# A Perceiver block on one core: first residual's norm folded into centered weights, table roots in the last batch, and side steps in another order

## The chip, the core and the metric

The kernel runs on one core of a Trainium2 chip. The metric is the device time of one execution in microseconds (us). The engines are named as in the profile: PE multiplies matrices (PEld loads its weights, beside it), DVE is the vector engine, ACT the scalar engine with its function tables, POOL and SP issue little work here beside DMAs. All data are 32-bit floats.

## The reference, cut to what matters

There are four batches of 256 tokens with 256 channels, and a context of 4096 tokens with 192 channels for each batch.

```
x = x + xattn(layernorm(x), ctx)    # 16 heads of 16, 256 queries against 4096 keys
x = x + attn(layernorm(x))          # 16 heads, q and k normed per head, causal softmax, 256 x 256
x = x + ffn(layernorm(x))

attn(h): k, q, v = h @ Wk.T, h @ Wq.T, h @ Wv.T, cut into heads
         q, k = headnorm(q)*g + b, headnorm(k)*g + b   # (t - mean) * rsqrt(var + 1e-5) over a head's 16
         softmax(q k^T / 16, causal) @ v @ Wo.T + bo
ffn(h):  logits = (gelu([h, slot_mean] @ w1 + b1) @ w2 + b2) / (|tau| + 0.1)
         alpha = softmax over the best 8 of 64 slots, 0 elsewhere
         si = (alpha^T h) / (sum of alpha + 1e-8)        # 64 slots x 256
         S = GRU(si, slots)                              # gates r, z, n
         y = S + softmax(q k^T / 8) v                    # attention of the 64 slots, one head
         (alpha @ (norm(y) @ wvp)) @ wo + bo
layernorm(x): (x - mean) / sqrt(var + 1e-5) over 256 channels
```

## The kernel before

`fast_` keeps a hand-written order for PE, DVE and ACT; each engine runs its instructions as written and stalls where an operand is late. The eight PSUM banks are four pairs (`two`), and each slot takes them in rotation as `w, x_, y, z`.

The loop runs over `b` from 0 to 4. For b = 0 to 3 it walks the context of batch b in slots `p`, each of which handles two blocks of 128 keys: `cross_block` multiplies keys with queries (L181) into the four pairs and takes the exponentials on ACT (L1666 and L1668), and one step later `cross_weigh` multiplies them with the values (L195) and DVE adds the result to `sums` (L1680). While batch b is in cross attention, all that follows cross attention for batch b-1 runs as side work: the dictionary `plan[b, p, i]` puts a function into slot p at one of five places, and `take(i, ...)` calls it with PSUM banks. Functions that `yield` go on at the next `later()`. Slot 6 of each batch from 1 on is the self attention (`SELF_AT`): two `self_block` calls and no cross attention. Slots 4 to 14 of b = 0 hold the weights' preparation (`set_plain` and so on). Even slots prepare the next keys, odd ones the next values.

At b = 4 there is no cross attention left. The side work of batch 3 runs alone, step after step, and the last steps of batch 2 (`slot_mix`, `slot_values`, `give`) stand among it. So that PE is not idle there, `fill` issues multiplications of zeros (L1052) whose number is set in `WAITS`: for each slot, us ahead of `take(1)` and us at the slot's end, at 0.43 us each.

Steps that the change touches:

- `cross_out` adds the first residual; its continuation is `norm` (statistics L958 and L959, then `rsqrt`, then the application L965). `rsqrt` is a bit trick (L943) and three Newton rounds of three instructions (L947 to L949), all on DVE. `x1_turned` transposes the normed x1 on PE (L980) and copies it on DVE (L986); `qk` multiplies it with the weights (L992), copies it and squares it on ACT, sums the squares on DVE (L1291), takes the roots and scales the heads (L1300). `qk_turned` transposes (L1318) and applies gain and offset on DVE (L1327, L1338). `self_values` copies its product on DVE (L166).
- `self_block` takes exponentials (L1703) and multiplies each tile's diagonal with the causal mask on DVE (L1705), right behind them.
- `normed_x` of the next batch stands at slot 5, `queries` at slot 14, with both halves in one bank.
- `routing` finds the best eight on DVE (L1393, L1394) and takes exponentials (L1399); `gates` are the GRU's products (L992) and elementwise work; `slot_qkv`, `slot_scores`, `at_turned` stand at slots 14, 15, 16; `slot_mix` (L1515, L1523, L1525), `slot_values` (product L992, then L1545) and `give` (L1551, L1559, output DMA L1560) at slots 5, 6 and 9 of the batch after, and behind the loop for batch 3.

Of the kernel before, what the change touches and what calls it, by code (L numbers as in the profile page):

```python
# [20 lines left out]
P = 128  # L21
# [11 lines left out]
CLAMP = 10000.0  # L33
MASKED = -1e30
# [11 lines left out]
    1: (0.4, 4.3),  # L46
    2: (0.4, 0.0),
    3: (0.0, 5.2),
    6: (0.0, 0.43),
    7: (0.0, 0.86),  # L50
    8: (0.4, 2.6),
    9: (0.0, 0.43),
    10: (0.0, 0.43),
    11: (0.0, 2.6),
    12: (0.0, 0.43),
    13: (0.0, 1.7),
    15: (0.0, 0.86),
}

# [853 lines left out]
def fast_(es, tc, nc, a, out, k, const, x0):  # L913
# [23 lines left out]
    def rsqrt(v):  # L937

        p, n = v.shape
        y = small.tile([P, n], F32, name="rs_y", tag=f"rs_y{n}")[0:p]  # L940
        t = small.tile([P, n], F32, name="rs_t", tag=f"rs_t{n}")[0:p]
        nc.vector.tensor_scalar(v, v, EPS, None, ALU.add)
        nc.vector.tensor_scalar(  # L943
            y.bitcast(I32), v.bitcast(I32), -0.5, 1597463007.0, ALU.mult, ALU.add
        )
        for _ in range(3):
            nc.vector.scalar_tensor_tensor(t, y, -0.5, y, ALU.mult, ALU.mult)  # L947
            nc.vector.tensor_tensor(t, t, v, ALU.mult)
            nc.vector.scalar_tensor_tensor(y, t, 1.5, y, ALU.add, ALU.mult)  # L949
        return y  # L950

    def norm(src):
# [7 lines left out]
        nc.vector.tensor_copy(var, mv[:, :, 1])  # L960
        rs = rsqrt(var)
# [54 lines left out]
    def queries(s, bank):  # L1016


        for c in range(2):
            product(  # L1020
                bank[:, c * NQ : (c + 1) * NQ],
                lambda m: k.wq[:, m, c * P : (c + 1) * P],
                lambda m: s.xnT[:, m, :],
            )
        qh = qp.tile([P, 2, 2, NQ], F32, name="qh", tag="qh")
        for c in range(2):
            q = bank[:, c * NQ : (c + 1) * NQ]
            nc.vector.tensor_scalar(
                qh[:, c, 0, :], q, k.bq[:, c : c + 1], pscale[:, 0:1], ALU.add, ALU.mult
            )  # L1030
            nc.scalar.activation(
                qh[:, c, 1, :], q, AF.Identity, bias=bqodd[:, c : c + 1], scale=pscale[:, 1:2]
            )
        s.qh = qh.rearrange("p c e q -> p c (e q)")
# [3 lines left out]
    for b, s in enumerate(batches):  # L1038
        s.b = b
# [78 lines left out]
    def set_plain(bank):  # L1118
# [13 lines left out]
        for v in vself:  # L1132
            ones_beside(nc, v)

# [93 lines left out]
    def set_centered(bank):  # L1228

        nc.vector.memset(sumto, 1.0 / C)  # L1230
# [27 lines left out]
    def cross_out(s, bank):  # L1258
# [9 lines left out]
        apply = norm(x1)  # L1268
        yield
        yield  # L1270
        s.x1n = halves(temp())
        apply(s.x1n)
        nc.gpsimd.tensor_tensor(x1, x1, abo.unsqueeze(1).to_broadcast([P, QT, C]), ALU.add)

    def x1_turned(s, bank):
        s.x1nT = turned(bank, s.x1n)
        s.qk = [temp() for _ in range(QT)]
        s.var = small.tile([P, QT * 2 * H], F32, name="var", tag="var")

    def qk(s, t, bank):  # L1280
        product(
            bank,
            lambda c: s.x1nT[:, c, t * P : (t + 1) * P],
            lambda c: wqkv[:, c, 0 : 2 * C],
        )
        nc.scalar.copy(s.qk[t], bank)
        sq = temp()
        nc.scalar.activation(sq, bank, AF.Square)
        yield
        var = s.var[:, t * 2 * H : (t + 1) * 2 * H]  # L1290
        nc.vector.tensor_reduce(var, sq.rearrange("p (h d) -> p h d", d=D), AX.X, ALU.add)  # L1291
        if t == 1:
            nc.vector.tensor_scalar(s.var, s.var, 1.0 / D, None, ALU.mult)
            rs = rsqrt(s.var)
            yield
            yield
            for u in range(QT):
                f = s.qk[u].rearrange("p (h d) -> p h d", d=D)
                r = rs[:, u * 2 * H : (u + 1) * 2 * H]
                nc.vector.tensor_tensor(  # L1300
                    f, f, r.unsqueeze(2).to_broadcast([P, 2 * H, D]), ALU.mult
                )

    def self_values(s, bank):
        for t in range(QT):
            product(
                bank[:, t * C : (t + 1) * C],
                lambda c: s.x1nT[:, c, t * P : (t + 1) * P],
# [3 lines left out]
        spread_values(nc.vector.tensor_copy, s.vself, halves(bank))  # L1312

    def qk_turned(s, i, bank):

        for c in range(2):
            for t in range(QT):
                nc.tensor.transpose(  # L1318
                    bank[:, (2 * c + t) * P : (2 * c + t + 1) * P],
                    s.qk[t][:, i * C + c * P : i * C + (c + 1) * P],  # L1320
# [3 lines left out]
        if i == 0:  # L1324
            q = held.tile([P, 2, 2, NQ], F32, name="sq", tag="sq", bufs=1)
            for e in range(2):
                nc.vector.tensor_scalar(  # L1327
                    q[:, :, e, :],
                    src,
                    gb[:, e : e + 1],  # L1330
                    gb[:, 2 + e : 3 + e],
                    ALU.mult,
                    ALU.add,
                )
            s.sq = q
        else:
            s.sk = held.tile([P, 2, NQ], F32, name="sk", tag="sk", bufs=1)
            nc.vector.tensor_scalar(s.sk, src, gb[:, 4:5], gb[:, 5:6], ALU.mult, ALU.add)  # L1338
# [6 lines left out]
    def self_out(s, bank):  # L1345
# [9 lines left out]
        apply = norm(s.x2)  # L1355
# [14 lines left out]
    def routing(s, bank):  # L1370

        for t in range(QT):
# [7 lines left out]
        lg, rest, best = (  # L1380
            small.tile([P, QT, n], F32, name=name, tag=name)
            for name, n in (("lg", SLOTS), ("rest", SLOTS), ("best", 8))
# [9 lines left out]
        for t in range(QT):  # L1392
            nc.vector.max(best[:, t, :], lg[:, t, :])  # L1393
            nc.vector.match_replace(rest[:, t, :], best[:, t, :], lg[:, t, :], -3.0e38)  # L1394
        nc.vector.tensor_scalar(top, best[:, :, 0], -1.0, None, ALU.mult)
        yield
        for t in range(QT):
            for x, acc in ((lg, None), (rest, None), (best, asum[:, t : t + 1])):
                nc.scalar.activation(  # L1399
                    x[:, t, :], x[:, t, :], AF.Exp, bias=top[:, t : t + 1], accum_out=acc  # L1400
# [3 lines left out]
        nc.vector.tensor_tensor(lg, lg, rest, ALU.subtract)  # L1404
# [38 lines left out]
    def gates(s, bank, other):  # L1443

        for i, to in ((0, bank), (2, other), (1, other)):
            for m in range(2):
                product(
# [426 lines left out]
```

## Time and profile before

| | |
|---|---|
| three timed runs | 903.44, 904.85, 906.26 us, median 904.85 |
| the profiled execution's own time | 904.43 us |
| its span, first to last instruction | 902.6 us |
| PE busy | 866.2 us, 96% of the span |
| ACT busy | 592.1 us, 66% |
| DVE busy | 328.8 us, 36% |
| last product with values of batch 3 ends | about 819 us |
| last result written by DVE | 895.95 us |

Busy time of PE counts the multiplications of zeros too. The stretch up to about 820 us is the four batches' cross attention with side work; the stretch from there to the end is batch 3's side work alone. An instruction of the small kind (a column or two of 128 rows) takes 0.15 to 0.18 us on DVE, and the next begins about 0.2 us after it.

### The profile page before, as it was taken

The page shows a single profiled execution, that of the slowest core. Times are in us where ns is not written, and L with a number is a line of the kernel's source. Part 1 is how long each engine was busy: PE and PEld are TensorE (multiplying, and loading weights), DVE is VectorE, ACT ScalarE, POOL GpSimd, SP SyncE. Part 2 cuts the span into 40 slices and gives each one's busy share as a digit, 9 for nine tenths or more (in the row PEclk, how much of TensorE's full clock was granted, in tenths as well). Part 3 has the DMA queues.
Part 4 walks back from the last instruction along what each step waited for, and adds up shares of the span by engine and source line. Part 5 has one row for each costly group of instructions (what it writes and reads, how often), then busy time and mean ns, then how long its engine had stood idle before and what let it go on. Part 6 is the DMA issues. An engine that isn't in the chain of part 4 may idle for free.

```text
span 902.6 us, 18933 instructions
## 1 busy us (share of the span) xinstructions
PE 866.2 (96%) x8143; PEld 467.1 (52%) x8143; DVE 328.8 (36%) x872; ACT 592.1 (66%) x838; POOL 18.0 (2%) x21
## 2 busy tenths in 40 slices
PE   8999999999999999999998999999999999998884
PEld 5444545545454555545444545545545545545663
DVE  3134222223346423223346423222445333224753
ACT  3777766766776787676774778767776678662310
POOL 1000000000000100000000000000000000000000
PEclk9999999999999999999999999999999999999997
DMA  7502110000000000000000000000000000000000
GB/s 194 122 25 60 36 48 25 25 20 6 24 24 25 25 25 24 25 25 21 5 25 24 25 29 10 23 25 25 24 25 25 10 27 25 1 1 1 1 12 17
DMA packets 21757, 25.71 MB, mean 28 GB/s; under 512 B 6496, under 2 KB 13216, under 8 KB 21664
## 3 DMA queue, kind: packets, MB, share of 16 engines
q1 hardware_dynamic: 20992, 23.88, 9.3%
q8 instruction: 66, 1.08, 0.5%
q10 hardware_dynamic: 576, 0.52, 0.2%
q14 instruction: 27, 0.22, 0.1%
q0 software_dynamic: 96, 0.01, 0.0%
HBM read 23.35 MB, written 1.05 MB: 27 GB/s over the span
## 4 chain that ended last, share of the span: by engine, by line
PE 89%; DVE 6%; ACT 3%; issue 1%; ACTq 0%; DVEq 0%
PE banks L181 28%; PE banks L195 25%; PE banks L992 8%; PE banks L96 6%; PE banks L123 6%; PE banks L136 4%; PE banks L102 4%; ACT prob L1668 2%; PE banks L980 1%; PE banks L1052 1%; PE banks L1722 1%; PE banks L1693 1%; PE banks L210 1%; DVE prob L1705 1%; PE banks L1415 1%
## 5 line engine op out<-in xcount | busy, mean ns | idle before, releaser
L1668 ACT ACTIVATE prob<-banks 128x1024 f32<-128x1024 f32 x384 | 366.6, 1043 | 0.0
L181 PE MATMUL banks<-qh,kt 32*128 32x512 f32 x2048 | 271.0, 623 | 3.3 <-ACT prob L1668 1.8
L195 PE MATMUL banks<-prob,v 128*32 128x256 f32 x4096 | 234.3, 381 | 2.8 <-ACT prob L1668 1.9
L1666 ACT ACTIVATE prob<-banks 128x512 f32<-128x512 f32 x256 | 139.0, 595 | 134.4 <-PE banks L181 134.4
L195 PEld LDWEIGHTS banks<-prob,v 128*32 128x32 f32 x4096 | 126.5, 110 | 126.8 <-ACT prob L1666 46.0
L181 PEld LDWEIGHTS banks<-qh,kt 32*128 32x128 f32 x2048 | 105.8, 184 | 122.8 <-issue 72.5
L1680 DVE TENSOR_TENSOR sums<-banks,sums 128x512 f32<-128x512 f32 x120 | 82.6, 690 | 200.9 <-PE banks L195 180.0
L123 PE MATMUL banks<-wv,ctx 128*128 128x256 f32 x256 | 62.3, 386 | 0.2
L96 PE MATMUL banks<-ctx,wk 128*128 128x512 f32 x128 | 61.4, 602 | 0.0
L123 PEld LDWEIGHTS banks<-wv,ctx 128*128 128x128 f32 x256 | 46.1, 190 | 13.1 <-ACT prob L1666 4.4
L166 DVE COPY v<-banks 128x512 f32<-128x512 f32 x35 | 23.9, 690 | 77.4 <-PE banks L136 77.4
L110 DVE TENSOR_SCALAR kt<-banks,bk 128x512 f32<-128x512 f32 x32 | 24.0, 750 | 53.3 <-PE banks L102 53.3
L111 ACT ACTIVATE kt<-banks,bk 128x512 f32<-128x512 f32 x32 | 22.0, 687 | 31.1 <-PE banks L102 30.9
L1703 ACT ACTIVATE prob<-banks 128x512 f32<-128x512 f32 (+1 forms) x40 | 24.1, 691 | 21.0 <-PE banks L1693 21.0
L166 ACT COPY v<-banks 128x512 f32<-128x512 f32 x29 | 17.0, 586 | 31.7 <-PE banks L136 31.1
L1052 PE MATMUL banks<-idle 128*128 128x256 f32 x134 | 34.8, 406 | 2.2 <-DVE idle L1047 1.5
L136 PE MATMUL banks<-wv,ctx 64*128 64x256 f32 x256 | 36.3, 402 | 0.0
L102 PE MATMUL banks<-ctx,wk 64*128 64x512 f32 x128 | 36.1, 641 | 0.0
L96 PEld LDWEIGHTS banks<-ctx,wk 128*128 128x128 f32 x128 | 21.3, 190 | 18.5 <-ACT prob L1668 10.6
L1052 PEld LDWEIGHTS banks<-idle 128*128 128x128 f32 x134 | 26.3, 205 | 7.0 <-DVE idle L1047 1.5
L136 PEld LDWEIGHTS banks<-wv,ctx 64*128 64x128 f32 x256 | 22.0, 186 | 11.3 <-issue 9.9
L986 DVE COPY tmp<-banks 128x512 f32<-128x512 f32 x21 | 14.5, 691 | 31.2 <-PE banks L980 30.0
(213 smaller groups left out, 555.0 us busy)
## 6 DMA issues: line engine op xcount, KB each, us to landing
ctx<-in_ctxT SPq DMA_DIRECT2D x32, 256.0 KB, 3.1
ctx<-in_ctxT SPq DMA_DIRECT2D x64, 128.0 KB, 3.3
x<-in_x SPq DMA_DIRECT2D x4, 256.0 KB, 4.1
out<-tmp SPq DMA_DIRECT2D x4, 256.0 KB, 2.5
wih<-in_ffn_WihT SPq DMA_DIRECT2D x1, 768.0 KB, 6.6
tmp<-in_ffn_WhhT SPq DMA_DIRECT2D x3, 256.0 KB, 4.7
wq<-in_L_xattn_Wq ACTq DMA_DIRECT2D x1, 256.0 KB, 4.0
wo<-in_L_xattn_Wo SPq DMA_DIRECT2D x1, 256.0 KB, 4.9
```

Source lines behind the costliest of these rows:

```text
L96: nc.tensor.matmul(pk[c], k.wk[:, 0, c * P : (c + 1) * P], cx[:, 0, :], start=True, stop=False)
L102: nc.tensor.matmul(pk[c], k.wk[left(c), 1, c * P : (c + 1) * P], cx[left(c), 1, :], start=False, stop=True,)
L123: nc.tensor.matmul(pv[n // 2][:, n % 2, :], cx[:, 0, n * P : (n + 1) * P], k.wv[:, 0, :], start=(n % 2 == 0), stop=False, skip_group_check ...
L136: nc.tensor.matmul(pv[u][:, i, :], cx[left(u), 1, n * P : (n + 1) * P], k.wv[left(u), 1, :], start=False, stop=True, skip_group_check=True,)
L166: copy(v[:, :, 0 : H * VW].rearrange("p i (h w) -> p i h w", w=VW)[:, :, :, 0:D], src.rearrange("p i (h d) -> p i h d", d=D),)
L181: nc.tensor.matmul(sc[:, m, :], kt[r, c, i * P : (i + 1) * P], qh[r, c, :], start=True, stop=True)
L195: nc.tensor.matmul(po[q * 32 : (q + 1) * 32, s * NQ : (s + 1) * NQ], v[:, i, w0 : w0 + 32], pr[s][:, m, e * NQ : (e + 1) * NQ], start=(fir ...
L992: nc.tensor.matmul(dst, lhs(c), rhs(c), start=(c == 0), stop=(c == 1))
L1052: nc.tensor.matmul(bank[:, 0:NQ], idle[:, 0:P], idle[:, 0:NQ], start=True, stop=True)
L1666: nc.scalar.activation(pt[:, m, :], sc[:, m, :], AF.Exp)
L1668: nc.scalar.activation(pt, sc, AF.Exp)
L1680: nc.vector.tensor_tensor(s.sums[c], po[:, c, :], s.sums[c], ALU.add)
```

## The change

The first residual is no longer normed ahead of its products. `set_inputs`, new in slot 5 of b = 0, takes each column's mean off the query, key and value weights, so that a row's mean drops out of the products. What is left of the norm is one factor per row: in q and k it cancels against the heads' norm if that norm's epsilon is scaled by the row's variance (`epsx`), and in v it is applied where the values are copied (`rs1`). `x1_turned` therefore transposes x1 itself. The statistics and the Newton rounds are still taken, in `cross_out`.

In the last batch the roots of the heads' norm, the norm of x2 and the slots' norm come from ACT's table (`AF.Sqrt`, then a reciprocal on DVE).

The squares are taken before the copy; the second half of q's gain, k's gain and the values' copy go to ACT. The masks move behind the weighing and its sums. `routing`, `gates`, `slot_qkv` (in the last batch the values' product gets its own bank) and `slot_mix` are reordered. `normed_x` moves to slot 9, `queries` to 11 and 15 (one half each), `slot_scores` to 14, `at_turned` to 15, `slot_mix` to 16 of the same batch, `slot_values` to 3, `give` to 5. The last `give` uses two banks and two DMAs, the second from ACT. The fills of the tail are set anew; 67 in all become 52.

```
 WAITS = {
...
-    1: (0.4, 4.3),
-    2: (0.4, 0.0),
-    3: (0.0, 5.2),
-    6: (0.0, 0.43),
+    1: (0.43, 0.43),
+    2: (0.43, 0.0),
+    3: (0.0, 2.15),
+    6: (0.0, 0.86),
...
-    8: (0.4, 2.6),
+    8: (0.43, 2.6),
...
-    11: (0.0, 2.6),
+    11: (0.0, 2.15),
...
-    13: (0.0, 1.7),
-    15: (0.0, 0.86),
+    13: (0.0, 1.3),
+    14: (0.43, 0.86),
 }
+LAST_WAIT = 0.43
...
+    def rsqrt(v, by_table=False):
...
+        if by_table:
+            nc.scalar.activation(y, v, AF.Sqrt)
+            nc.vector.reciprocal(y, y)
+            return y
...
-        nc.vector.tensor_copy(var, mv[:, :, 1])
-        rs = rsqrt(var)
+        nc.vector.tensor_scalar(var, mv[:, :, 1], EPS, BIG, ALU.add, ALU.min)
+        return mv, var
...
+    def queries(s, c, bank):
+        q = bank[:, 0:NQ]
+        product(q, lambda m: k.wq[:, m, c * P : (c + 1) * P], lambda m: s.xnT[:, m, :])
...
+    def set_inputs(bank, other):
+
+        for to, cols in ((bank, slice(0, 2 * C)), (other[:, 0:C], slice(2 * C, 3 * C))):
+            product(to, lambda c: sumto, lambda c: wqkv[:, c, cols])
+            for c in range(2):
+                nc.vector.tensor_tensor(wqkv[:, c, cols], wqkv[:, c, cols], to, ALU.subtract)
...
         nc.vector.tensor_tensor(x1, halves(bank), s.xo, ALU.add)
         yield
-        apply = norm(x1)
-        yield
-        yield
-        s.x1n = halves(temp())
-        apply(s.x1n)
-        nc.gpsimd.tensor_tensor(x1, x1, abo.unsqueeze(1).to_broadcast([P, QT, C]), ALU.add)
+        _, var = moments(x1)
+
+        s.eps = small.tile([P, QT], F32, name="epsx", tag="epsx")
+        nc.vector.tensor_scalar(s.eps, var, EPS, None, ALU.mult)
+        s.rs1 = rsqrt(var)

     def x1_turned(s, bank):
-        s.x1nT = turned(bank, s.x1n)
-        s.qk = [temp() for _ in range(QT)]
+        s.x1T = turned(bank, s.xo)
...
-        nc.scalar.copy(s.qk[t], bank)
         sq = temp()
         nc.scalar.activation(sq, bank, AF.Square)
+        nc.scalar.copy(s.qk[:, t, :], bank)
         yield
...
+        nc.vector.tensor_scalar(var, var, 1.0 / D, s.eps[:, t : t + 1], ALU.mult, ALU.add)
         if t == 1:
-            nc.vector.tensor_scalar(s.var, s.var, 1.0 / D, None, ALU.mult)
-            rs = rsqrt(s.var)
+            if s.last:
+                nc.vector.tensor_scalar(s.var, s.var, BIG, None, ALU.min)
+            rs = rsqrt(s.var, s.last).rearrange("p (t i h) -> p t i h", t=2, i=2)
+            if s.last:
+                preload(AF.Exp)
...
-        spread_values(nc.vector.tensor_copy, s.vself, halves(bank))
+        for t in range(QT):
+            spread_values(
+                lambda dst, src: nc.scalar.activation(
+                    dst, src, AF.Identity, scale=s.rs1[:, t : t + 1]
+                ),
...
-            for e in range(2):
-                nc.vector.tensor_scalar(
...
+            nc.vector.tensor_scalar(
+                s.sq[:, :, 0, :], src, gb[:, 0:1], gb[:, 2:3], ALU.mult, ALU.add
+            )
+            nc.scalar.activation(
+                s.sq[:, :, 1, :], src, AF.Identity, bias=gb[:, 3:4], scale=gb[:, 1:2]
+            )
...
-            nc.vector.tensor_scalar(s.sk, src, gb[:, 4:5], gb[:, 5:6], ALU.mult, ALU.add)
+            nc.scalar.activation(s.sk, src, AF.Identity, bias=gb[:, 5:6], scale=gb[:, 4:5])
...
-        apply = norm(s.x2)
+        apply = norm(s.x2, s.last)
...
-        for i, to in ((0, bank), (2, other), (1, other)):
...
+        gate(0, bank)
         nc.vector.tensor_tensor(r, by_half(bank, 0), gh[:, 0], ALU.add)
         nc.scalar.activation(r, r, AF.Tanh, scale=0.5)
-        nc.vector.tensor_tensor(z, by_half(other, 2), gh[:, 1], ALU.add)
-        nc.scalar.activation(z, z, AF.Tanh, scale=0.5)
+        gate(4, other)
...
+        gate(2, bank)
+        nc.vector.tensor_tensor(z, by_half(bank, 2), gh[:, 1], ALU.add)
         yield
...
         nc.scalar.activation(n, n, AF.Tanh)
+        nc.scalar.activation(z, z, AF.Tanh, scale=0.5)
...
-        s.rsy = rsqrt(mv[:, 1:2])
+        nc.vector.tensor_scalar(mv[:, 1:2], mv[:, 1:2], EPS, BIG, ALU.add, ALU.min)
+        s.rsy = rsqrt(mv[:, 1:2], s.last)
...
-            plan[b - 1, 5, 4] = step(normed_x, s)
+            plan[b - 1, 9, 4] = step(normed_x, s)
             plan[b - 1, 10, 1] = step(x_turned, s)
-            plan[b - 1, 14, 1] = step(queries, s)
+            plan[b - 1, 11, 1] = step(queries, s, 0)
+            plan[b - 1, 15, 1] = step(queries, s, 1)
...
-            ((14, 0), step(slot_qkv, s)),
-            ((15, 0), step(slot_scores, s)),
-            ((16, 0), step(at_turned, s)),
+            ((14, 2 if s.last else 0), step(slot_qkv, s)),
+            ((14, 1), step(slot_scores, s)),
+            ((15, 0), step(at_turned, s)),
+            ((16, 2), step(slot_mix, s)),
...
-            ((5, 2), step(slot_mix, s)),
-            ((6, 1), step(slot_values, s)),
-            ((9, 3), step(give, s)),
+            ((3, 1), step(slot_values, s)),
+            ((5, 0), step(give, s)),
...
             if own:
+                self_masks(first)
                 if not s:
                     fill(w[:, 1, :], SELF_WAIT)
                 prs = (first, self_block(prev, 1, (x_, y, z, w)))
+                self_masks(prs[1])
...
+    plan[B + 1, 3, 1](banks[:, 0, :])
+    fill(banks[:, 1, :], LAST_WAIT)
+    plan[B + 1, 5, 0](banks[:, 2, :], banks[:, 3, :])
```

## The prediction, made before the changed kernel ran

> **What bounds the kernel now.** I read the page first, then PE's waits, the chain of waits over the last 110 us, and a table of stretches of 3.41 us, the step in which the granted clock changes. The page:
>
> ```profile
> span 902.6 us, 18933 instructions
> PE 866.2 (96%) x8143; PEld 467.1 (52%) x8143; DVE 328.8 (36%) x872; ACT 592.1 (66%) x838; POOL 18.0 (2%) x21
> PE 89%; DVE 6%; ACT 3%; issue 1%; ACTq 0%; DVEq 0%
> ```
>
> PE bounds the kernel as a whole. Up to 820 us it waits for nearly nothing, so a shorter DVE chain there brings only what PE stood still for. PE's waits, with total, count and longest:
>
> ```profile
> PE banks L1693 <- DVE sums L1680: 4.2, 2, 3.1
> PE banks L1551 <- ACT prob L1668: 2.3, 2, 1.1
> PE banks L1523 <- ACT prob L1668: 1.1, 2, 0.6
> ```
>
> After 820 us the chain changes hands at every step. Its pieces, with start and duration:
>
> ```profile
> 829.66 0.88 PE banks L980 x4
> 830.57 0.70 DVE tmp L986
> 831.31 3.71 PE banks L992 x8
> 844.30 1.62 PE banks L1693 x16
> 853.46 2.84 PE banks L1722 x64
> 866.69 0.88 PE banks L980 x4
> 893.08 2.08 PE banks L1551 x4
> 895.26 0.69 DVE tmp L1559
> ```
>
> A start that moves earlier here moves the end. In the following rows the busy times of PE, PEld, DVE, ACT and POOL are followed by the granted clock:
>
> ```profile
> 483.04:486.45 3.41, 1.40 (x5) 0.77 (x6) 3.41 (x8) 1.01 (x3) 0.00 (x0) 1.00 0.00 0
> 486.45:489.86 3.41, 3.41 (x9) 2.23 (x9) 1.55 (x3) 0.58 (x1) 0.00 (x0) 0.50 0.00 0
> 814.13:817.54 3.41, 1.91 (x36) 1.20 (x40) 0.00 (x0) 2.37 (x3) 0.00 (x0) 1.00 0.02 5
> 865.33:868.74 3.41, 1.83 (x9) 1.09 (x9) 3.18 (x11) 0.00 (x0) 1.27 (x1) 1.00 0.06 22
> 868.74:872.15 3.41, 3.41 (x12) 2.61 (x11) 1.34 (x5) 1.76 (x2) 0.00 (x0) 0.50 0.15 55
> ```
>
> A stretch with PE busy for 1.83 us or less is followed by one at half clock; after 1.91 us none follows. There are four such dips: from 486.45, 803.89, 868.74 and 892.63 us. The same L992 products take 3.64 us in the first and 1.99 elsewhere; four of L1551 take 2.08 at the end and 1.13 in a full-clock batch. So a dip costs PE up to 1.7 us.
>
> **Part by part, to 820 us.**
>
> *Queries in two banks*: before, the first scores wait 1.51 us for a key copy (L110) queued behind the queries' copies. One small DVE instruction goes and the two halves no longer follow each other: −0.9, bounds −1.5 and 0.
>
> *set_inputs* adds PE work once: two products of 128x512 at 0.93 us and two of 128x256 at 0.48 are +2.8. Its four DVE subtractions (2 x 0.69 + 2 x 0.42 = 2.2 us) lie beside cross attention.
>
> *Self attention's order*: before, L1693 waits 1.06 and 3.11 us for sums (L1680), which on DVE stand behind masks (L1705, 2.5 us), Newton rounds (3.6 us) and the slots' norm. Masks now follow the sums, normed_x goes to slot 9, and both waits go: −4.2. With them goes the dip from 486.45: 3.64 − 1.99 = −1.65. What is late next is the masks' reader, the weighing of the second self block, with a block's scores between.
>
> *give and slot_mix*: give waited twice 1.14 us for ACT; at slot 5 it reads nothing late: −2.3. In slot_mix y now comes first, and y's bank waits about 1.15 us for the exponential instead of 0.57: +1.1 over two batches. slot_scores in slot 14 stands behind exponentials for fq and fk: +0.25 in each of three: +0.7. The last slot_mix, in slot 16, falls into a wait of 1.88 us (813.75 to 815.63) for ACT, but y cannot start before about 814.65, so it pushes the weighing to 816.5: +0.9.
>
> *ACT's new work*: half of q's gain, k's gain and the values' copy are 0.69 + 0.69 + 2 x 0.47 = 2.3 us more per batch among exponentials, in three batches. ACT is 66% busy, and PE waits for it only a few us; I take 0, with bounds 0 and +7.
>
> Sum: −0.9 + 2.8 − 4.2 − 1.65 − 2.3 + 1.1 + 0.7 + 0.9 = −3.6.
>
> **The tail**, as shifts of a start from before's time, each including those ahead of it.
>
> *First residual.* Of the norm only the application (0.42 us, and its handoff) and the wait for it leave the path. The statistics and the Newton rounds still stand on DVE between the residual (L1266) and the transposes' copy (L986), 16 small instructions, because `rs1` and `epsx` are made there. The products L992 start at 829.9 instead of 831.31: −1.4. But the fills here shrink from ten to one, so PE stands still from 826.9 to 829.9.
>
> By the trace's rows (under 1.83 us busy in a stretch) a dip follows, under L992 (3.71 us): +1.5. [...] I take the trace, where 2.0 us idle in a stretch was enough: cumulative 0.1.
>
> *Heads' root.* Newton's nine instructions and what stands around them take 837.12 to 839.88. In their place: a minimum 0.2, the root on ACT about 0.31, a reciprocal 0.55. The values' copy stands ahead of the second reduction on DVE (+0.97, less what the earlier Square wins). L1300 starts about 837.4 instead of 839.91, −2.5 without the dip.
>
> Each switch of the table is a load. The trace shows one, and the next instruction 0.02 us after it:
>
> ```profile
> 743.77 1.28 ACT L1368 ACT_TABLE_LOAD   x1
> 745.07 0.47 ACT L1368 ACTIVATE hT<-banks,b1c 128x256 f32<-128x256 f32 x1
> ```
>
> The load for the root can run behind the copy (834.8 to 836.05), before the variance is there at 836.35; the load back to exponentials lies under L1300 and the transposes. [...]
>
> *Gains.* q's halves split over DVE and ACT share a bank and follow each other, then k's gain on ACT: before L1327 and L1338 took 2.26 us serially. Gains and transposes give 1.0: scores start at 840.8 instead of 844.30, −3.5 without the dip. *Values' copy on ACT*: L166 (0.61 us, behind three masks on DVE) no longer holds up L1722: 848.7 instead of 853.46, −4.7.
>
> *Second residual's norm.* Twelve DVE instructions (863.85 to 866.18) become one, plus a root of about 0.22 and a reciprocal of 0.15: −6.5. PE now hardly idles before L980 of x2, so the dip from 868.74 goes and L992 falls from 1.72 to 1.03 with L1373 likewise: −7.7.
>
> *Routing, gates, slots*: routing −0.1; in gates z's tanh stands behind n's: +0.4; slot_qkv and slot_scores about +0.1: −7.3 in all.
>
> *Slots' norm*: the 2.3 us of Newton before sv (892.55) go; what is late next is the w3·yT product: −9.0.
>
> *Last give*: two banks, each with its own sum and DMA; at full clock 1.13 us instead of 2.08, and the first DMA leaves after 0.43 us of DVE instead of 0.69. −10.8. Behind the last DVE result (895.95) SP issues the DMA and the program's end takes 6.65 us; that remains.
>
> Tail: −10.8 + 1.5 (dip at x1) = −9.3. In gates and routing PE may dip again, with three fills for 1.5 us of idle: 0.3 x 1.3 = +0.4. So −8.9.
>
> Total: −3.6 − 8.9 = −12.5. The profiled execution took 904.43 (span 902.6 and 1.8 around it), so 891.9. It lies 0.4 below the median of 904.85; I forecast for the median: 892.3.
>
> **The rivals.**
>
> *ACT in order gives the main stages back* (chance 0.2). For it: the 2.3 us per batch lie ahead of exponentials in ACT's order, and PE already waits 1.8 and 1.9 us for L1668. Against: ACT has a third of its time free. At its bound of +7: 899; the half of it 896.
>
> *Stronger gain* (0.1). The x1 gap causes no dip, and the waits in slot_mix and slot_scores are filled by PE work behind them: −1.5 − 2.7 − 0.4, so 887.7.
>
> *The norm's folding does nothing* (part of the likeliest). Its statistics and roots stay ahead of the copy, so of some 4 us only 1.4 are saved; that is in the sum. If DVE's order put them behind the copy, 3 us more would go (889).
>
> *The tail at half clock* (slower, 0.04). 15 fills go, and if with them each stretch of the tail fell under 1.83 us busy, all PE pieces on the chain, some 29 us after removing fills, would take twice their time: +29 − 13 = +16, 921. The point from which it decides: with −12.5 to lose and 1.5 to 1.7 a dip, eight dips on the path. For it: one is certain by the rows. Against: only three of the tail's stretches were that idle before, and the same change shortens the idle times.
>
> *Little difference* (0.03): ACT's bound and a few dips together, 902 to 907.
>
> **How the numbers follow.** The likeliest, 0.63: 888 to 896 by the bounds of the unknown costs (queries ±0.9, slot_mix ±2, dips ±1.5[...]). The range takes the half of ACT's rival and most of the stronger gain: 886.5 to 898. About 0.3% (2.7 us) is what a measurement of this kernel can tell from no change. Faster: 0.63 + 0.2 + 0.1 = 0.93; same 0.03; slower 0.04.
>
> **What would show it.** Right: L1693 waiting for sums under 0.5 us; L1551 waiting for ACT no more; no half clock near 486; in the tail 3 us idle ahead of x1's L992 followed by half clock; two more table loads of 1.28 us, both ended before their readers' data; L1722 starting about 5 us earlier relative to L980; none of Newton's rows behind x1. Wrong: PE waiting for ACT in slots 7 to 16 by more than 5 us over before's; half clock in more than four stretches after 820 us; a pause of over 1 us behind a table load.

## The result, and the profile after

| | before | after |
|---|---|---|
| timed runs, us | 903.44, 904.85, 906.26, 906.39 | 889.44, 889.98, 892.16, 893.15 |
| median, us | 905.56 | 891.07 |
| profiled execution, us (span) | 904.43 (902.6) | 889.44 (887.7) |
| last addition to `sums` starts, us | 819.36 | 812.39 |
| from there to the end of the span, us | 83.2 | 75.3 |

The ratio is 0.9845, with a 95% interval of 0.9815 to 0.9875. The forecast was 892.3. The median fell by 14.5 us. Of the 14.9 us that the span lost, 7.0 went in the four batches' cross attention and 7.9 behind it.

The page of the changed kernel: span, busy times, and the chain by engine.

```profile
span 887.7 us, 18875 instructions
PE 858.0 (97%) x8121; PEld 460.7 (52%) x8121; DVE 316.0 (36%) x823; ACT 605.9 (68%) x862; POOL 18.0 (2%) x21
PE 93%; ACT 3%; DVE 3%; issue 1%; ACTq 0%; DVEq 0%
```

DVE is on the chain for 3% instead of 6%, PE for 93% instead of 89%. PE's waits (total, count, longest):

```profile
PE banks L1003 <- DVE tmp L997: 5.0, 4, 4.0
PE banks L1547 <- ACT prob L1709: 3.5, 3, 1.2
PE banks L183 <- ACT prob L1709: 1.9, 1, 1.9
```

The 4.2 us for sums and the 2.3 us of the last product for ACT are gone. New are 4.0 us ahead of x1's products, and ahead of slot_mix's y (L1547) there are three waits of 1.2 us instead of two of 0.6.

The chain in the last batch, with start and duration:

```profile
819.84 1.19 DVE ln_v L966
823.05 0.61 DVE tmp L997
823.70 6.16 PE banks L1003 x12
831.50 0.26 ACT rs_y L945
836.16 1.64 PE banks L1734 x16
844.21 2.78 PE banks L1764 x64
855.65 0.88 PE banks L991 x4
880.85 1.29 PE banks L1588 x4
882.16 0.43 DVE tmp L1596
```

The first row is unexpected: an instruction of 128x2 takes 1.19 us instead of 0.17. The third holds eight products of the row's queries and keys and four of other work; it contains a stretch at half clock, as this table of stretches shows (busy us of PE, PEld, DVE, ACT, POOL, then the granted clock):

```profile
819.82:823.24 3.42, 0.00 (x0) 0.00 (x0) 3.05 (x13) 0.00 (x0) 1.17 (x1) 1.00 0.00 0
823.24:826.65 3.41, 2.95 (x4) 1.40 (x5) 0.41 (x1) 0.00 (x0) 0.00 (x0) 0.50 0.00 0
874.43:877.84 3.41, 2.68 (x17) 1.42 (x16) 1.48 (x8) 1.36 (x2) 0.00 (x0) 1.00 0.01 2
877.84:881.26 3.42, 3.42 (x7) 1.61 (x8) 0.77 (x3) 0.20 (x1) 0.00 (x0) 0.50 0.00 0
```

The first dip (a stretch at half clock) is the one forecast. The second is not: it follows a stretch in which PE was busy for 2.68 us.

### The profile page after: what moved, and what is told of

It reads as the page before. It is cut to its first block, busy times and chain, and to the rows that moved or that the text cites. A ratio compares the mean times of both kernels' runs of the same rounds, so it can differ in the third digit from the quotient of the medians.

```text
span 887.7 us, 18875 instructions
## 1 busy us (share of the span) xinstructions
PE 858.0 (97%) x8121; PEld 460.7 (52%) x8121; DVE 316.0 (36%) x823; ACT 605.9 (68%) x862; POOL 18.0 (2%) x21
## 3 DMA queue, kind: packets, MB, share of 16 engines
q8 instruction: 65, 1.06, 0.5%
## 4 chain that ended last, share of the span: by engine, by line
PE 93%; ACT 3%; DVE 3%; issue 1%; ACTq 0%; DVEq 0%
PE banks L183 29%; PE banks L197 26%; PE banks L1003 9%; PE banks L98 6%; PE banks L125 6%; PE banks L104 4%; PE banks L138 4%; PE banks L1057 2%; PE banks L991 1%; ACT prob L1709 1%; PE banks L1764 1%; PE banks L1734 1%; PE banks L212 1%; PE banks L1441 1%; ACT prob L1744 0%
## 5 line engine op out<-in xcount | busy, mean ns | idle before, releaser
L1057 PE MATMUL banks<-idle 128*128 128x256 f32 x104 | 29.8, 425 | 2.2 <-DVE idle L1052 1.5
L1744 ACT ACTIVATE prob<-banks 128x512 f32<-128x512 f32 (+1 forms) x40 | 23.9, 693 | 10.1 <-PE banks L1734 10.1
L1003 PE MATMUL banks<-wqkv,tmp 128*128 128x512 f32 (+1 forms) x64 | 24.7, 523 | 4.5 <-DVE tmp L997 4.0
L997 DVE COPY tmp<-banks 128x512 f32<-128x512 f32 x21 | 14.5, 692 | 37.4 <-PE banks L991 37.4
```

The source lines that it names most:

```text
L1003: nc.tensor.matmul(dst, lhs(c), rhs(c), start=(c == 0), stop=(c == 1))
L1057: nc.tensor.matmul(bank[:, 0:NQ], idle[:, 0:P], idle[:, 0:NQ], start=True, stop=True)
```

## The experiments

Each is an edit of the changed kernel, whose median is 891.07. Times are medians of the timed runs (four to six each), and the ratio is that to the kernel before. Each run also has a mean granted clock. Within one kernel the time follows it, which is used below: the changed kernel took 889.44 at a clock of 0.994, 889.98 at 0.993, 892.16 at 0.990 and 893.15 at 0.988. The kernel before, timed again beside these runs, had medians from 904.74 to 906.32, so a difference of 1.5 us or less between two medians is not shown by them alone.

| kernel | median, us | runs from to | ratio to before (95%) |
|---|---|---|---|
| Newton in the last batch | 897.46 | 896.44 to 900.09 | 0.9902 to 0.9933 |
| masks and normed_x in the old order | 897.05 | 895.01 to 899.96 | 0.9898 to 0.9935 |
| x1's gap filled | 890.37 | 886.86 to 890.61 | 0.9824 to 0.9850 |
| copy ahead of statistics | 886.13 | 883.25 to 887.54 | 0.9759 to 0.9797 |
| x1 normed first | 893.61 | 889.39 to 895.35 | 0.9825 to 0.9873 |
| gains and values on DVE | 894.96 | 894.68 to 897.14 | 0.9872 to 0.9902 |
| yT ahead of y | 888.94 | 885.60 to 889.98 | 0.9791 to 0.9825 |
| waits of the main stages filled | 889.18 | 888.81 to 889.52 | 0.9802 to 0.9829 |
| POOL behind a POOL copy | 894.71 | 891.10 to 895.38 | 0.9856 to 0.9896 |
| POOL behind a DVE copy | 891.61 | 887.76 to 893.59 | 0.9815 to 0.9871 |
| all that helped | 881.57 | 880.71 to 881.77 | 0.9723 to 0.9750 |

### Newton in the last batch

```
-        if by_table:
+        if False:
...
-            if s.last:
-                preload(AF.Exp)
```

> The changed kernel with the roots of the last batch taken by Newton rounds again (heads' norm, norm of x2, slots' norm), all else as changed. My theory: each of the three roots stood on the path, and the tables took 2.5 (heads), 2.2 (x2) and 2.3 us (slots) off it, so about +7 us against the changed kernel (about 898), +8 if PE idles long enough ahead of x2's transposes for a half-clock stretch. Rival: [...]what the tables brought was small, and this kernel is only +2 to +4 us slower.

Measured: +6.4. In the profiled executions the stretch from the last addition to `sums` to the end is 81.5 us against 75.3, so 6.2 us lie behind cross attention. In it are three half-clock stretches that the changed kernel lacks (two from 839.2, one from 866.5, behind PE's wait ahead of x2's transposes, which the expectation had named), and the one from 877.84 is missing. At the same clock of 0.988 the two kernels took 897.11 and 893.15, +4.0. PE's waits give the roots' own share: for the scaled heads it waits 2.7 us instead of 0.9, ahead of x2's transposes 2.1 instead of 0.6, and for the slots' norm 1.0 instead of nothing. That is 1.8 + 1.5 + 1.0 = 4.3 us and not 7.0; the rest is dips. The 2.5 for the heads was the prediction's shift with the first residual's 1.4 in it; as steps of their own the prediction has −1.1, −1.8 and −1.7, −4.6 in all, which agrees. The rival's number fits. No table load lies on the changed kernel's path: the roots' loads of 1.28 us start at 829.98, 844.40 and 874.52, and the roots at 831.50, 854.74 and 878.01.

Its profile shows something more. Up to its last batch its code is that of the changed kernel, yet its execution has half-clock stretches there that the other has not. Stretches around the same wait of 1.9 us for ACT, first of the Newton kernel:

```profile
794.87:798.28 3.41, 1.56 (x12) 0.72 (x14) 0.22 (x1) 3.12 (x4) 0.00 (x0) 1.00 0.00 0
798.28:801.69 3.41, 3.41 (x24) 0.94 (x20) 0.00 (x0) 3.21 (x5) 0.00 (x0) 0.50 0.00 0
801.69:805.11 3.42, 3.42 (x40) 1.59 (x36) 0.59 (x1) 0.32 (x1) 0.00 (x0) 0.50 0.00 0
```

then of the changed kernel:

```profile
795.93:799.34 3.41, 2.05 (x14) 0.98 (x16) 0.00 (x0) 3.12 (x5) 0.00 (x0) 1.00 0.00 0
799.34:802.76 3.42, 3.42 (x57) 1.63 (x58) 0.58 (x1) 2.94 (x4) 0.00 (x0) 1.00 0.00 0
```

The stretches of 3.41 us do not start with the program. In one execution the wait lay within one stretch, which left 1.56 us of work in it, and two stretches at half clock followed. In the other a stretch boundary cut into it, 2.05 us of work were left, and none followed. The last addition to `sums` began 4.4 us later (816.83 against 812.39).

### Masks and normed_x in the old order

```
...
                     nc.scalar.activation(pt[:, g, 0:n], sc[:, g, 0:n], AF.Exp)
+        self_masks(pr)
         return pr
...
-                self_masks(first)
...
-                self_masks(prs[1])
...
-            plan[b - 1, 9, 4] = step(normed_x, s)
+            plan[b - 1, 5, 4] = step(normed_x, s)
```

> The changed kernel with the causal masks right behind the exponentials again and the next batch's norm of x in slot 5 again, all else as changed. My theory: PE waits again for DVE's sums ahead of the self attention's second scores in the batches 1 and 2 (4.2 us in all) and the second of these waits brings the half-clock stretch back (+1.65): about +5.9 us (about 897). Rival: the half-clock stretch hangs on where the 3.41 us stretches happen to fall, not on this order: +3 to +4.2 and no half clock between 470 and 500 us. A third: slot_mix, which also stood on DVE ahead of those sums, was the cause, and is elsewhere now: +0 to +2.

Measured: +6.0, the first theory's number, but not by its parts. PE waits for sums again, 0.9 us twice, and not 4.2 in all:

```profile
PE banks L1734 <- DVE sums L1721: 1.7, 2, 0.9
```

Together with what hangs on it, the self attention costs 1.5 us more in each of batches 1 and 2. The other 3.3 us in the profiled execution are two half-clock stretches, from 402.7 and 610.8 us, behind the 1.15 us wait of slot_mix and not near 486. As the second expectation had it, no half clock came between 470 and 500 us. The third was partly right: in the kernel before, slot_mix's norm stood on DVE ahead of the masks and sums for 2.1 us (479.14 to 481.26), which the change took away, and the wait there is 0.9 instead of 3.11 us. At the first of the two waits, where no slot_mix stood, it is 0.9 instead of 1.06.

### x1's gap filled

```
-    2: (0.43, 0.0),
+    2: (3.87, 0.0),
```

> The changed kernel with eight more fills in the gap of 3.96 us in which PE waits for the transposed x1 (3.44 us of multiplications of zeros, nothing else). My theory: the gap causes the half-clock stretch after it, under which four products of L1003 take 0.85 instead of 0.43 us each. With the fills the clock stays at 1.00 and the end comes 1.5 to 1.7 us earlier (about 889.5). Rival: the fills only push the products back or the products' reader (DVE, then ACT) was late anyway: 0 to +0.5.

Measured: −0.7. In its profile the dip is gone (clock 1.00 from 820 to 830 us, 0.82 and 0.84 in the two halves of this for the changed kernel), and L1773, the addition behind the self attention, begins 1.4 us earlier than in the changed kernel, with the same start of the tail. That execution, at a clock of 0.998, took 886.86. The other four ran at 0.993 and took 890.08 to 890.61: their clock suggests dips elsewhere, which no profile shows. The dip's cause is shown, its worth in the median isn't.

### Copy ahead of statistics

```
         nc.vector.tensor_tensor(x1, halves(bank), s.xo, ALU.add)
         yield
+        if s.last:
+            yield
+            yield
+            yield
         _, var = moments(x1)
...
         s.rs1 = rsqrt(var)
+        if s.last:
+            add_bias(s)
...
         s.x1T = turned(bank, s.xo)
-        nc.gpsimd.tensor_tensor(
-            s.xo, s.xo, abo.unsqueeze(1).to_broadcast([P, QT, C]), ALU.add
-        )
+        if not s.last:
+            add_bias(s)
```

`add_bias` holds the POOL addition that stood there.

> The changed kernel in which, in the last batch alone, the statistics and Newton rounds of x1 come behind the copy of the transposed x1 (and POOL's addition behind them). My theory: the folded norm brings little only because these 14 DVE instructions still stand ahead of that copy; with the copy first the products start about 3.7 us earlier, the half-clock stretch goes too (1.5), and the heads' variances are then held up by the statistics for about 1 us: -4 to -5 us (about 886.5). Rival: the statistics only move ahead of the first reduction of the squares, which needs them, and the wait moves with them: 0 to -1.5.

Measured: −4.9. From its chain:

```profile
823.84 0.69 DVE tmp L997
824.53 0.34 DVE ln_st L964
835.90 1.64 PE banks L1744 x16
```

The copy is now ahead of the statistics, and the scores (L1744) start 19.0 us after the last addition to `sums` (816.88), where the changed kernel needs 23.8: 4.8 less, of which 1.5 are the dip under x1's products. This is the first expectation, not the rival.

### x1 normed first

```
-        _, var = moments(x1)
...
-        s.rs1 = rsqrt(var)
+        apply = norm(x1)
+        s.x1n = halves(temp())
+        apply(s.x1n)
...
-        s.x1T = turned(bank, s.xo)
+        s.x1T = turned(bank, s.x1n)
```

> The changed kernel with the first residual normed ahead of its transposes again (its result times centered weights; the row's factor and the scaled epsilon fall away), all else as changed. By the prediction's own term the folding is worth 1.4 us once the last batch is alone: +1.4. My theory after the first traces: POOL's addition to x1, which the folded form lets start while DVE still takes the statistics, holds up one DVE instruction for 1.0 us (1.18 instead of 0.17), and that eats the gain: +0.3 us (0 to +0.6), with L966 back at 0.17 us and x1's L1003 about as late as in the changed kernel.

Measured: +2.5 in the median, outside the 0 to +0.6 expected, but the runs fall in two groups: 889.39 and 890.26 at clocks of 0.995 and 0.994, three at 893.61 to 895.35 below 0.988. At 0.994 the changed kernel took 889.44 and this one 890.26. In the profile x1's L1003 begins 12.2 us after the last `sums` against 11.3; of the difference 0.55 is a dip that here also covers the transposes (1.22 us instead of 0.67). L966 is back at 0.17 us. So as it stands in the changed kernel the folding is worth some tenths. That is what POOL leaves of it: from the start of the residual's addition to x1's products it takes 6.6 us here, 6.1 without that dip, and 4.86 in the folded kernel whose POOL keeps away ("POOL's addition to x1", second attempt). By itself the folding is thus worth about 1.2 us, near the prediction's 1.4.

### Gains and values on DVE

```
-            nc.scalar.activation(s.sk, src, AF.Identity, bias=gb[:, 5:6], scale=gb[:, 4:5])
+            nc.vector.tensor_scalar(s.sk, src, gb[:, 4:5], gb[:, 5:6], ALU.mult, ALU.add)
...
```

The second half of q's gain and the scaled copy into `vself` are changed likewise.

> The changed kernel with q's second gain, k's gain and the scaled copy of the values on DVE instead of ACT, all else as changed. My theory: ACT's 2.3 us per batch cost nothing up to 812 us, and in the last batch the three gains follow each other on two engines as they do on one (0.82 + 0.78 + 0.68), so 0 to +1 us, the +1 where the values' copy falls behind the masks on DVE. Rival of the prediction (ACT gives the main stages back): this kernel is 2 to 7 us faster.

Measured: +3.9, which neither had. PE's waits have a row that is in neither kernel:

```profile
PE banks L183 <- DVE vself L1335: 3.6, 3, 1.2
```

The copy that empties the values' bank stands on DVE behind sums and all eight masks (in the first self attention these take 4.89 us from 278.47, and the copy starts at 283.28), and cross attention's next scores need that bank. With the masks moved behind the weighing, the copy on ACT is part of what makes the new order work. PE waits for neither gain in the main stages. The rival of the prediction, in which ACT gives time back, is refuted.

### yT ahead of y

```
+        for f in (to_y, to_yT) if s.last else (to_yT, to_y):
+            f()
```

`to_y` and `to_yT` hold the products as they were.

> The changed kernel in which slot_mix of the batches 0 to 2 issues the products for yT (whose bank is free) ahead of those for y again, all else as changed. My theory: y's bank is free only after an exponential, PE stands still for 1.15 us there in each of three batches, and 0.58 us of yT's work fits in: −1.7 us, and somewhat more where these waits had brought half-clock stretches (they lie in other places from run to run). Rival: the weighing behind it waits for the same exponentials anyway: 0.

Measured: −2.1. The wait at this place falls from 3.5 to 1.7 us:

```profile
PE banks L1547 <- ACT prob L1715: 1.7, 3, 0.6
```

### Waits of the main stages filled

```
             take(0, x_[:, 0, :])
+            if p == 16 and 0 < b < B:
+                fill(x_[:, 1, :], 0.86)
             take(2, x_[:, 0, :], y[:, 1, :])
+            if p == 15 and b == B - 1:
+                fill(x_[:, 1, :], 1.72)
```

> The changed kernel with fills (multiplications of zeros) in three kinds of waits of the main stages: 0.86 us ahead of slot_mix in the last slot of batches 1 to 3, 1.72 us at the end of batch 3's slot 15. My theory: the runs of one kernel differ because the half-clock stretches fall on these waits in some runs and not in others; with the waits filled the granted clock of every run is at 0.994 or above and the runs lie within 1.5 us of each other, their median 1 to 2 us under that of the changed kernel. Rival: the fills delay what follows, or the differences have another cause: the same spread (889 to 893) or slower.

Measured: −1.9, and all five runs lie between 888.81 and 889.52 at a clock of 0.994. The changed kernel's lie between 889.44 and 893.15. So the differences between the runs of the changed kernel are most likely half-clock stretches behind these waits, present in some executions and not in others. The profiles say the same: of seven kernels whose code up to the last batch is the same but for a few small instructions, four (Newton, copy ahead of statistics, x1 normed first, POOL behind a DVE copy) were profiled with such stretches behind the wait of 1.9 us, and three (the changed kernel, x1's gap filled, POOL behind a POOL copy) without. The profiled execution is as long up to the last batch, within 0.4 us, as the changed kernel's, which happened to have none of them.

### POOL's addition to x1

POOL adds a bias to x1 as soon as the transposes and the second statistics have read it, and DVE's slow L966 starts at 819.84, beside it:

```profile
819.73 1.26 POOL L1288 TENSOR_TENSOR xo<-xo,abo 128x512 f32<-128x512 f32 x1 [96.52 <-DVE ln_st L964]
```

L966 ends at 821.02 and POOL's addition at 820.99. The first attempt to part them:

```
         s.x1T = turned(bank, s.xo)
+        late = small.tile([P, QT], F32, name="late", tag="late")
+        nc.gpsimd.tensor_copy(late, s.rs1)
         nc.gpsimd.tensor_tensor(
```

> The changed kernel with one small POOL instruction that reads the row factors ahead of POOL's addition to x1, so that the addition starts only when the Newton rounds are done. My theory: the addition and DVE's L966 (128x2, 1.18 us beside it and 0.17 us in the other eleven places) get in each other's way; apart from each other, L966 takes 0.17 again and x1's products, with all behind them, start 1.0 us earlier; the end comes about 1 us earlier where the half-clock stretches lie alike. Rival: L966 waits for something else, such as the second statistics: it stays at 1.18 us and the time is the same.

It did not do this: POOL took the addition first (its small instruction ran at 823.1), and L966 stayed at 1.18. So it tests neither theory. Its median is 3.6 us higher, its profiled execution (891.15) 1.7 us. Ahead of x2's root ACT stood idle for 10.4 us until L966 was done (854.8) and only then loaded the table, where the changed kernel had loaded it at 844.40. Why the wait came ahead of the load here was not shown. From its chain:

```profile
854.83 1.28 ACT L945
856.12 0.21 ACT rs_y L945
```

The load stands on the path with its full 1.28 us (the root follows 0.01 us after it), and PE's wait ahead of x2's transposes grows from 0.6 to 1.9 us. Two half-clock stretches follow in the tail (857.4 and 871.1), where the changed kernel has the one from 877.84. What the slower runs hold beyond this no profile shows. The second attempt:

```
         s.rs1 = rsqrt(var)
+        seen = small.tile([P, QT], F32, name="seen", tag="seen")
+        nc.vector.tensor_copy(seen, x1[:, 0, 0:QT])
```

> The changed kernel with one 128x2 copy out of x1 on DVE behind the Newton rounds, so that POOL's addition, which overwrites x1, has to wait for it (in the run before, POOL took its small instruction after the addition, and nothing moved). My theory: L966 of the last batch falls from 1.18 to 0.17 us because POOL no longer works beside it; the added copy costs 0.2; x1's products start 0.8 us earlier after the residual, and the end comes 0.8 us earlier where half-clock stretches lie alike. Rival: L966 stays at 1.18 us: it waits for something else, and the time rises by 0.2. Another: POOL then holds up the copy L997 (0.69 us) instead, and nothing is gained.

Here POOL adds at 826.11, after the last Newton instruction. The rows for L966 of the changed kernel and of this one (minimum, median, maximum in ns):

```profile
L966 DVE TENSOR_SCALAR ln_v<-ln_mv x12: 169/170/1178, 5.6 to 854.5; 128x2 f32<-128x2 f32 x12
```

```profile
L966 DVE TENSOR_SCALAR ln_v<-ln_mv x12: 169/170/172, 5.7 to 857.7; 128x2 f32<-128x2 f32 x12
```

From the start of the residual's addition (L1278) to x1's products it takes 4.86 us (821.75 to 826.61) instead of 5.79 (817.91 to 823.70): −0.9 with an instruction more. The copy L997 (825.87 to 826.56), beside POOL for its last 0.45 us, kept its 0.69 us. In the time it shows only at like clocks: 887.76 at 0.994 against 889.44, one run each; the median of 891.61 has three runs at 0.990 and 0.988 above it.

### All that helped

The edits of "copy ahead of statistics", "yT ahead of y" and "waits filled" (0.43 instead of 0.86 us ahead of slot_mix), and x1's root by table:

```
-        s.rs1 = rsqrt(var)
+        s.rs1 = rsqrt(var, s.last)
...
         if s.last:
+            preload(AF.Sqrt)
             yield
```

> All that helped, together: copy of the transposed x1 ahead of its statistics in the last batch, these statistics' root by table too (its table loaded early), yT ahead of y in slot_mix of the batches 0 to 2, fills of 0.43 us ahead of slot_mix and of 1.72 us in batch 3's slot 15. My theory: the gains add up, as they lie in different places: copy first took 4.9, yT first 2.1, the fills 1.9 (overlapping with yT by 1 or so), and the root another 0.5 to 1 us off the variances of the heads: 881 to 883 us, with all runs at a clock of 0.994 or above. Rival: the gains were half-clock stretches counted twice: 885.

Measured: 881.57, 9.5 us under the changed kernel and 23 under the one before. The runs lie 1.1 us apart, at clocks of 0.998 and 0.999. In its profile no stretch is at half clock before its last results. That is within the 881 to 883 expected, but not by all of its parts: the table for x1's root was not run alone, and the scores start 18.7 us after the last addition to `sums`, against 19.0 with the copy first, so it brought 0.3 us and not 0.5 to 1.

## Why the prediction was right, and where it was not

**The sum** said −12.5; the profiled executions differ by 15.0 and the medians by 14.5. Up to 820 us 3.4 us more went than forecast, behind it 1.0 less, so the total is nearer than the first of its parts; to that extent it was luck. The range of 886.5 to 898 held the median.

**Self attention's order.** The waits for sums went (4.2 to 0), and so did the dip near 486: between the self attentions of batches 1 and 2 the kernel gained 3.9 us. But masks and normed_x, moved back alone, bring back only 1.7 of the 4.2; nearly all of the rest is slot_mix's move (2.2 at the second wait). The prediction had named the slots' norm among what stood ahead of the sums, without a share.

**give and slot_mix.** give's 2.3 us went as forecast. y waits 1.15 us as forecast, three times. slot_scores' +0.7 did not show: no wait of its own appears. set_inputs cost 2.78 us, the forecast's 2.8. The queries' wait fell from 1.51 to 0.93 us, −0.6 instead of −0.9.

**What the forecast left out up to 820 us**: −7.0 instead of −3.6. Some 1.5 us of this are the dip from 803.89 of the profiled execution before (three such stretches cost the Newton kernel 4.4 us). The prediction counted it among the four and gave it no term; the changed kernel's execution, in which the stretches lay elsewhere, had none there, and the Newton kernel's had three. Part of this difference is thus chance and not the change. With slot_scores' 0.7 less and the queries' 0.3 more, about 1.5 us are left that no run accounts for.

**ACT's new work: 0, with bounds 0 and +7.** The number was near, the reasoning failed: the move is needed. On DVE these instructions cost 3.9 us.

**First residual: −1.4.** Measured −0.6 (11.95 to 11.31 us from the last `sums` to the products). The term missed 1.0 us of POOL beside DVE; without it the folding is worth about what was forecast. That the statistics stay ahead of the copy was right, and the 3 us put down for the opposite order were, with the dip, 4.9. The dip under these products came as the trace's rows said: four products took 3.3 us instead of 1.8, behind a gap of 3.96 us, and with the gap filled there was no dip. But the border that the prediction drew, 1.83 us busy, does not hold in other rows (last section); for the x1 gap, with PE idle through a whole stretch (0.00 us busy from 819.82 to 823.24), it made no difference.

**Heads' root: −2.5 without the dip.** Of the shift at the scores, −2.0 was forecast with the dip and −1.2 measured; the difference is POOL's. The loads of the table were hidden: the root's ran from 829.98 to 831.26, the variance came at 831.48 and the root started at 831.50; the load back, from 831.77 to 833.05, ended long before the exponentials (837.32). The sum of the prediction has nothing for the loads, and no pause behind them shows: the instruction behind the load back starts 0.02 us after it. The root took 0.26 us instead of the 0.31 put down, its reciprocal the 0.55.

**Values' copy and x2's root.** L1722 became L1764, forecast −4.7 + 1.5 = −3.2, measured −2.3. At x2's transposes −5.0 was forecast and −4.1 measured, and the dip that stood behind them is gone. Both keep the error of 0.8 to 0.9 from x1.

**Last give: −9.3 with x1's dip, measured −6.4** at the last DVE result. The step that failed is "at full clock 1.13 us". A dip from 877.84 covers slot_values' product (1.93 us), the fill (1.15) and part of give (1.29); in the kernel with the copy first these are 1.08, 0.63 and 1.08. In the changed kernel that is 1.6 us more, and x1's error of 0.9 comes on top. The 0.4 put down for another dip was the right kind and too little.

**The end: 6.65 us "that remains"**, measured 5.1 (882.59 to 887.7). Before, SP issued the last DMA at 895.98, behind the last DVE result; now it issues the first of the two at 882.25, 0.34 us before the last result is written. With what belongs to the issue it is done 0.1 us after the last result instead of 0.8. Then it waits, first in the kernel before, then in the changed kernel (total, count, longest):

```profile
SPq L892 <- SPq L892: 3.6, 1, 3.6
SPq L894 <- SPq L894: 2.7, 1, 2.7
```

So the earlier issue is worth 0.7 us and the shorter wait 0.9; why the wait is shorter was not tested. These 1.6 us were not forecast, and they hide part of what the last give missed.

## What to carry to other kernels

When a step is folded into a later one, look at where its statistics stand in the engine's order, not only at what no longer depends on them: the folding alone brought 0.6 us here, and three `yield`s brought 4.9 us. Put something into waits of 1 to 2 us even if nothing waits behind them, since work that follows may pay for the idle time at half clock (filling them took 1.9 us off the median here, and the runs then lay 0.7 us apart instead of 3.7); and compare runs by their granted clock before a difference of 0.3% is put down to an edit. A move between engines is to be judged in the new order: the copy on ACT looked free, and with the masks moved it keeps them from stopping PE.

## What the runs showed of the hardware

- The half-clock stretches lie on a grid of 3.41 us: in the kernel before, 93, 19 and 7 of them lie between the dips from 486.45, 803.89, 868.74 and 892.63. The grid does not start with the program: carried back to the start of the span, its first boundary lies at about 1.8 us in the kernel before, 0.6 in the changed and 3.0 in the Newton kernel. A wait of 1.9 us was followed by two dips in one execution (from 798.28 in the Newton kernel) and by none in another of the same code (the changed kernel). Busy time alone does not decide: after 1.91 and 2.05 us none followed, but after 2.27 us (from 399.26 in the old-order kernel) and 2.68 us, both with slot_mix's small products among them, one did, and in the first attempt with POOL even after at least 2.7 (from 867.68; its products L1003 run from 868.39 past the stretch's end). Nor does little work always bring one. In the last batch of the Newton kernel a stretch with 1.66 us was followed by full clock, and only the one behind it, with 0.85, by half clock (from 829.00):

```profile
822.17:825.59 3.42, 1.66 (x9) 0.86 (x7) 3.06 (x8) 0.00 (x0) 1.26 (x1) 1.00 0.00 0
825.59:829.00 3.41, 0.85 (x2) 0.49 (x3) 2.19 (x12) 0.00 (x0) 0.00 (x0) 1.00 0.00 0
```

  What decides whether one follows was not settled.
- An addition of 128x512 on POOL (1.26 us) held up a DVE instruction of 128x2 (L966) by 1.0 us, until 0.03 us after POOL's end in the changed kernel. L966 took 1.18 us there and in the first attempt with POOL and 1.20 on the chain of the kernel with the copy first; it took 0.17 in the two kernels in which the addition came later (x1 normed first and the second attempt). A DVE copy of 128x512 out of PSUM beside the same addition (in the second attempt, for its last 0.45 us) kept its 0.69 us. Why POOL holds up the one and not the other was not shown.
- In these runs a table load was hidden where it stood ahead of the wait for its root's operand (829.98 to 831.26, operand at 831.48). Where ACT took that wait ahead of the load, in the first attempt with POOL, it cost its 1.28 us (854.83 to 856.11).
